# The hand-over to a recurrent stage: order of the early sigmoids, a PSUM bank, and who makes scale and shift

## The chip, the cores and the metric

The kernel runs on one core of a Trainium2 chip. The metric is device time in microseconds of one execution. A core has TensorE (PE, matrix products), VectorE (DVE), ScalarE (ACT, activations), GpSimd (POOL) and SyncE (SP, which issues transfers). Each engine works through its own queue in order. They meet through semaphores.

## The reference, cut to what matters

An image of 4 batches, 128 channels and 64 x 64 places passes an attention over places with a residual (layer 0), and then layer 1: a causal attention over 4096 tokens with layer norm, and a recurrent block. The change touches the recurrent block alone:

```
Wx   = layernorm(t) @ W.T                     # 4 batches x 4096 tokens x 128
Wx   = (Wx - mean) * rsqrt(var + 1e-5) * gamma + beta   # moments over all tokens of all batches
y    = 0
for each token:  y = sigmoid(Wx[token] + y @ V.T);  the output is t + y
```

## The kernel before

`fast_path` handles both layers. Nearly all of its time goes into the two attentions: products of scores (`s_ps`, L1062 and L1077), exponentials, products with values (`acc`, L1126 and L1137), one batch after another. The last block of the last batch is handled by `final_block`.

The recurrence is not run token by token. The 4096 tokens of a batch are cut into 256 chunks of 16 steps, and all chunks of a batch advance together: one step of one batch is one 128 x 256 product. A chunk's start is guessed: it is warmed up over the 9 tokens before it. Of these 9 steps, the first three (`AHEAD`) are "early": they run while the last block is still being finished, with moments over all blocks but the last one (`most`, made by `ahead`). The next six (`WARM`) and the 16 real steps use the moments over everything. At the end the kernel compares each chunk's guessed start with the true one and falls back to `general_path` if they differ.

An early step i of a batch has three instructions, each in a function of its own: `early_input` (L807: TensorE puts scale times Wx into PSUM), `early_product` (L812: adds V times the state), `early_sigmoid` (L820; for step 0 L822, straight from Wx). Batches 0, 1 and 2 take part whole, batch 3 without its last block (`WHOLE`). The last block's piece is 32 columns wide (`LAST`) and follows when its Wx is there. Results of early step 2 go to `warmed`, which lies in the tile `joint`. `early_place` says where in PSUM a step's sum lies: two tiles of two banks each, so four banks, with two halves of 256 columns in each. Before, a batch b uses bank b, and half i % 2 of it; the piece uses bank 3, and for step 2 bank 2.

The build makes an engine wait when another uses the same bank of PSUM, also for other columns of it.

`final_block` writes its order out by hand: `pin` keeps instructions in the order in which they are written. It mixes the early steps with the last block's own work: `normed_half`, `turned` (transposes), `product` (L994, with statistics at L995 on VectorE and a copy at L998 on ScalarE, which waits for these statistics).

After `final_block` come the moments over everything: `bn_aggr` (L1333), and `affine`, which makes the scale and the shift of the batch normalisation:

```
        nc.gpsimd.tensor_tensor(y, var, mhalf[:, :1], ALU.pow)
        nc.vector.scalar_tensor_tensor(z, in0=y, scalar=half, in1=y, op0=ALU.mult, op1=ALU.mult)
        nc.vector.scalar_tensor_tensor(y, in0=z, scalar=1.5, in1=y, op0=ALU.add, op1=ALU.mult)
        nc.vector.tensor_tensor(scale, y, gamma, ALU.mult)
        nc.vector.scalar_tensor_tensor(shift, in0=nmean, scalar=scale, in1=beta, op0=ALU.mult, op1=ALU.add)
```

GpSimd raises to the power -1/2, and one Newton step on VectorE makes it exact.

A later step of a batch is in `step`: a product `y_ps` (L1369; in step 0 L1374, in two parts, since the start of a chunk comes from the chunk before it), then VectorE's `z` = scale * Wx + y_ps (L1376), then ScalarE's sigmoid with the shift as its bias (L1380). Four batches are in flight. From step 1 on the order is pinned: batches 0 to 3, then the transposes for the output (`residual`, L1401) and the sums on GpSimd (`add`). The warm-up and step 0 are not pinned; a scheduler orders them at build time. `good` counts reciprocals that are in range; a copy of it into `count` (L1457) feeds the final verdict.

Of the kernel before, what the change touches and what calls it, by code (L numbers as in the profile page):

```python
# [9 lines left out]
F32 = mybir.dt.float32  # L10
AF = mybir.ActivationFunctionType
ALU = mybir.AluOpType
# [3 lines left out]
P = 128  # L16
# [3 lines left out]
BN_EPS = 1e-5  # L20
STEPS = 16
BY_C = 2
# [347 lines left out]
def fast_path(  # L370
# [22 lines left out]
    nc = tc.nc  # L393
    B, C, N = x.shape
# [101 lines left out]
    grid = lambda t: t.rearrange("p (g c) -> p g c", c=CPB)  # L496
    pin = tc.keep_in_program_order

    def affine(mv, pool, name, halved=True):

        one = lambda part: pool.tile([P, 1], F32, name=f"{name}_{part}")
        var, y, half, nmean, z = one("var"), one("y"), one("half"), one("nmean"), one("z")
        scale, shift, shift_half = one("scale"), one("shift"), halved and one("shift_half")
        nc.vector.tensor_scalar(var, mv[:, 1:2], BN_EPS, None, ALU.add)
        nc.gpsimd.tensor_tensor(y, var, mhalf[:, :1], ALU.pow)
        nc.vector.tensor_scalar(half, var, -0.5, None, ALU.mult)
        nc.vector.tensor_scalar(nmean, mv[:, 0:1], -1.0, None, ALU.mult)
        nc.vector.scalar_tensor_tensor(z, in0=y, scalar=half, in1=y, op0=ALU.mult, op1=ALU.mult)
        nc.vector.scalar_tensor_tensor(y, in0=z, scalar=1.5, in1=y, op0=ALU.add, op1=ALU.mult)
        nc.vector.tensor_tensor(scale, y, gamma, ALU.mult)  # L510
        if halved:
            nc.vector.scalar_tensor_tensor(
                shift_half, in0=nmean, scalar=scale, in1=beta_half, op0=ALU.mult, op1=ALU.add
            )
        nc.vector.scalar_tensor_tensor(shift, in0=nmean, scalar=scale, in1=beta, op0=ALU.mult, op1=ALU.add)
        return scale, shift, shift_half

# [10 lines left out]
    with tc.tile_pool(name="batch", bufs=1) as batch, tc.tile_pool(name="rows", bufs=2) as rowp, tc.tile_pool(  # L528
# [265 lines left out]
        def early_place(i, b, g0, g1):  # L794

            if not early:
                early.extend(halves.tile([P, 2, BLK], F32, tag="half", name="early") for _ in range(AHEAD - 1))
                early.extend(ps_s.tile([P, 2 * BLK], F32, tag="s", name="early_ps") for _ in range(2))
            cols = slice(g0 * CPB, g1 * CPB)
            bank, half = (b - 1, 1) if g0 and i == AHEAD - 1 else (b, i % 2)  # L800
            at = early[AHEAD - 1 + bank % 2][:, ds(bank // 2 * BLK + half * NCH, NCH)][:, cols]
            return cols, at, by_step[:, b, i - AHEAD - WARM + STEPS, g0:g1]

# [5 lines left out]
        def early_product(i, b, g0, g1):  # L809

            cols, at, _ = early_place(i, b, g0, g1)
            pin(nc.tensor.matmul(at, lhsT=vf, rhs=early_states(i - 1, b)[:, cols], start=False, stop=True))  # L812
# [125 lines left out]
        def final_block(b, g, agg, den):  # L938

            HALF = BLK // 2  # L940
            pair = lambda k: slice(2 * k, 2 * k + 2)
            token = lambda j: xs[:, b, ds(g * BLK + j * P, P)]
            own = folded(den, True, True)
            rec = recs[:, 1, b, ts(g, TPB)]
            pin(nc.vector.tensor_reduce(rec, own.rearrange("p q j -> p j q"), AX.X, ALU.add))
            pin(nc.vector.reciprocal(rec, rec))
            ops = [misc("o_ps"), misc("o_ps")]
            for j in range(TPB):
                pin(nc.tensor.matmul(ops[j // 2][:, ts(j % 2, P)], lhsT=agg[:, ts(j, P)], rhs=wv1, start=True, stop=True))

            st = stat.tile([P, TPB, nc.vector.BN_STATS_DIM], F32, tag="st", name="ln_st")
            mv = stat.tile([P, TPB, nc.vector.BN_AGGR_DIM], F32, tag="mv", name="ln_mv")
            var, y, half, z = (
                stat.tile([P, TPB], F32, tag=tag, name=f"ln_{tag}") for tag in ("var", "rstd", "half", "z")
            )
            for k in range(2):
                for j in range(2 * k, 2 * k + 2):
                    t = token(j)
                    pin(
                        nc.vector.scalar_tensor_tensor(  # L960
                            t, in0=ops[k][:, ts(j % 2, P)], scalar=rec[:, j : j + 1], in1=t, op0=ALU.mult, op1=ALU.add
                        )
                    )
                for j in range(2 * k, 2 * k + 2):
                    pin(nc.vector.bn_stats(st[:, j], token(j)))
                for j in range(2 * k, 2 * k + 2):
                    pin(nc.vector.bn_aggr(mv[:, j], st[:, j]))
                pin(nc.vector.tensor_scalar(var[:, pair(k)], mv[:, pair(k), 1], LN_EPS, None, ALU.add))
                pin(nc.gpsimd.tensor_tensor(y[:, pair(k)], var[:, pair(k)], mhalf[:, :2], ALU.pow))
                pin(nc.vector.tensor_scalar(half[:, pair(k)], var[:, pair(k)], -0.5, None, ALU.mult))  # L970
            by_tokens(b, g)

            xh = wk.tile([P, TPB, P], F32, tag="xh2", name="xh2")

            def normed_half(k):
                newton(y[:, pair(k)], half[:, pair(k)], z[:, pair(k)], True, True)
                j = 2 * k
                pin(nc.vector.tensor_scalar(xh[:, j], token(j), y[:, j : j + 1], None, ALU.mult))
                j += 1
                pin(nc.scalar.activation(xh[:, j], token(j), AF.Copy, scale=y[:, j : j + 1]))  # L980

            xhT = wk.tile([P, BLK], F32, tag="xhT2", name="xhT2")

            def turned(k):
                ps = misc("xh2T_ps")
                for i in range(2):
                    pin(nc.tensor.transpose(ps[:, ts(i, P)], xh[:, 2 * k + i], ident))
                pin(nc.vector.tensor_copy(xhT[:, ts(k, HALF)], ps[:, :HALF]))

            to = xs[:, b, ts(g, BLK)].rearrange("p (s c) -> p s c", s=STEPS)  # L990

            def product(k):
                wp = misc("wx_ps")[:, :HALF]
                pin(nc.tensor.matmul(wp, lhsT=wfc, rhs=xhT[:, ts(k, HALF)], start=True, stop=True))  # L994
                pin(nc.vector.bn_stats(ends[:, 3 + 6 * k : 9 + 6 * k], wp))  # L995
                part = pair(k)
                pin(
                    nc.scalar.copy(  # L998
                        to.rearrange("p s (q j u) -> p s q j u", q=Q, j=TPB)[:, :, :, part],
                        wp.rearrange("p (j q u s) -> p s q j u", q=Q, j=TPB // 2, s=STEPS),  # L1000
                    )
                )

            for part in WHOLE[:3]:
                early_step(1, part)
            normed_half(0)
            early_step(1, WHOLE[3])
            normed_half(1)
            early_step(2, WHOLE[0])
            turned(0)  # L1010
            early_input(2, *WHOLE[1])
            turned(1)
            early_product(2, *WHOLE[1])
            product(0)
            early_sigmoid(2, *WHOLE[1])
            early_input(2, *WHOLE[2])
            product(1)
            in_range(True)
            early_product(2, *WHOLE[2])
            early_input(2, *WHOLE[3])  # L1020
            early_product(2, *WHOLE[3])
            early_input(1, *LAST)
            early_input(2, *LAST)
            early_sigmoid(0, *LAST)
            for i in range(1, AHEAD):
                early_sigmoid(2, *WHOLE[1 + i])
                early_product(i, *LAST)
                early_sigmoid(i, *LAST)

# [279 lines left out]
    with tc.tile_pool(name="xr", bufs=1) as xrp, tc.tile_pool(name="y", bufs=2) as yp, tc.tile_pool(  # L1309
# [21 lines left out]

        mv = xrp.tile([P, nc.vector.BN_AGGR_DIM], F32, name="mv")
        nc.vector.bn_aggr(mv, ends)  # L1333
        scale, shift, _ = affine(mv, xrp, "all", False)
        start = xrp.tile([P, B, Q + 1, NCH // Q], F32, name="start")
        nc.gpsimd.memset(start[:, :, 0, 1:2], 0.0)
        ended = lambda b: start[:, b, 1:].rearrange("p q (g w) -> p g q w", g=NB)
# [58 lines left out]
        def residual(s):  # L1396
# [8 lines left out]
            pin(nc.vector.tensor_tensor(t, t, ps, ALU.add))  # L1405
            pin(nc.sync.dma_start(out=by_chunk(out_t)[:, :, s], in_=t))

        met = ps_m2.tile([P, BY_C, NCH], F32, name="met")
        gap = xrp.tile([P, B], F32, name="gap")
        tol = xrp.tile([P, B], F32, name="tol")  # L1410
# [4 lines left out]
        for s in range(-WARM, STEPS):  # L1415
            for b in range(B):
                step(b, s)
            if s >= 1:
                residual(s - 1)
            if TPB <= s < TPB + BY_C:  # L1420
                b = s - TPB
                pin(nc.scalar.copy(by_row(met[:, b]), ended(BY_C + b)))
            if 0 <= s < STEPS - 1:
                add(s)

# [27 lines left out]
        largest(1, second)  # L1453
        tc.mark_branch_hint_location(BRANCH, "LikelyTaken", engines=mybir.ALL_ENGINES)

        count = xrp.tile([P, B + 2], F32, name="count")
        nc.vector.tensor_copy(count[:, B:], good)  # L1457

        def judge():
            total = xrp.tile([P, 1], F32, name="total")  # L1460
# [87 lines left out]
```

## Time and profile before

| what | value |
|---|---|
| median of 3 runs | 2007.41 us (2006.56 to 2007.6) |
| the profiled execution | 2007.98 us, its span 2006.2 us |
| granted TensorE clock | 0.999 |
| TensorE busy | 1999.5 us (100% of the span) |
| VectorE, ScalarE, GpSimd busy | 1456.6, 974.5, 142.9 us |

The page gives busy time by engine, the chain of waits that ended last, and the costliest groups of instructions. A row of the timeline gives an instruction's start in us from the span's start, its length, engine, line and operands, how many were merged, and in brackets how long the engine stood idle before it and what ended that. PE and PEld are the product and the weight load of TensorE. A 32-bit product of 256 columns shows as two passes.

### The profile page before, as it was taken

Reading aid. Unit: us, or ns where it says so; the run is one execution under the profiler, and the core shown is the slowest. Engines: PE = TensorE matmul, PEld = TensorE weight load, DVE = VectorE, ACT = ScalarE, POOL = GpSimd, SP = SyncE. Lnnn points to the kernel's source line nnn. Section 1 sums busy time; section 2 is a strip of 40 time slices with the busy share of each in tenths; the row PEclk is TensorE's granted clock in tenths of the full one; section 3 lists DMA queues with packets and bytes.
Section 4 is the critical chain, followed back from the end, with each engine's and each line's share of the span. In section 5 each row is a group of like instructions: output and inputs, shape, how many; then the busy total and the mean of one; then the engine's idle time right before and its main releaser. Section 6 shows DMA issues by size and latency. Waiting matters only on the chain.

```text
span 2006.2 us, 31346 instructions
## 1 busy us (share of the span) xinstructions
PE 1999.5 (100%) x11862; PEld 873.2 (44%) x11862; DVE 1456.6 (73%) x2824; ACT 974.5 (49%) x1053; POOL 142.9 (7%) x253
## 2 busy tenths in 40 slices
PE   9999999999999999999999999999999999999999
PEld 3333354444333345444433334444443333544457
DVE  4799877555789987655588998664468998774469
ACT  5666633232666653333466664323356666333348
POOL 0000011000000001000000001000000000110016
PEclk9999999999999999999999999999999999999999
DMA  3111112310110111330102111222010111120018
GB/s 106 44 34 23 22 33 58 75 31 16 43 50 17 23 23 38 70 74 17 43 21 61 23 18 26 55 64 58 16 44 2 23 23 23 33 53 17 17 50 308
DMA packets 220027, 89.03 MB, mean 44 GB/s; under 512 B 142688, under 2 KB 204512, under 8 KB 219488
## 3 DMA queue, kind: packets, MB, share of 16 engines
q1 hardware_dynamic: 219584, 86.82, 17.5%
q8 instruction: 94, 1.54, 0.3%
q14 instruction: 61, 0.50, 0.1%
q10 hardware_dynamic: 288, 0.16, 0.0%
HBM read 45.84 MB, written 36.89 MB: 41 GB/s over the span
## 4 chain that ended last, share of the span: by engine, by line
PE 99%; DVE 0%; ACT 0%; issue 0%; POOL 0%; DVEq 0%; ACTq 0%; POOLq 0%
PE s_ps L1077 23%; PE acc L1137 22%; PE s_ps L1062 22%; PE acc L1126 22%; PE y_ps L1369 2%; PE o_ps L691 1%; PE r_ps L650 1%; PE kr_ps L587 1%; PE wx_ps L902 1%; PE v_ps L599 1%; PE o_ps L701 1%; PE yT_ps L1401 0%; PE early_ps L807 0%; PE warm_ps L544 0%; PE early_ps L812 0%; PE vT_ps L625 0%
## 5 line engine op out<-in xcount | busy, mean ns | idle before, releaser
L1106 DVE TENSOR_TENSOR dsum<-dsum,p 128x1024 f32<-128x1024 f32 x692 | 845.0, 1221 | 399.2 <-ACT p L1080 292.9
L1071 ACT ACTIVATE p<-s_ps,nshift 128x1024 f32<-128x1024 f32 x512 | 570.1, 1117 | 310.3 <-PE s_ps L1062 279.4
L1080 ACT ACTIVATE p<-s_ps 128x1024 f32<-128x1024 f32 (+2 forms) x288 | 274.5, 953 | 605.0 <-PE s_ps L1077 581.1
L1126 PE MATMUL acc<-p,v 64*64 64x512 f32 x4096 | 527.9, 589 | 0.0
L1062 PE MATMUL s_ps<-kr 64*64 64x512 f32 x2048 | 522.6, 590 | 0.0
L1062 PE MATMUL s_ps<-kr,swap 64*64 64x512 f32 x2048 | 522.6, 590 | 0.0
L1077 PE MATMUL s_ps<-rows,xhT 128*128 128x512 f32 (+3 forms) x1152 | 500.4, 558 | 0.0
L1137 PE MATMUL acc<-p,xh 128*128 128x512 f32 (+3 forms) x1152 | 500.2, 557 | 0.0
L1077 PEld LDWEIGHTS s_ps<-rows,xhT 128*128 128x128 f32 x1152 | 215.2, 190 | 243.1 <-issue 202.4
L1137 PEld LDWEIGHTS acc<-p,xh 128*128 128x128 f32 x1152 | 216.1, 190 | 239.8 <-issue 223.4
L1126 PEld LDWEIGHTS acc<-p,v 64*64 64x64 f32 x4096 | 156.6, 133 | 282.8 <-issue 274.6
L1062 PEld LDWEIGHTS s_ps<-kr,swap 64*64 64x64 f32 x2048 | 141.5, 133 | 140.6 <-issue 132.7
L1062 PEld LDWEIGHTS s_ps<-kr 64*64 64x64 f32 x2048 | 141.5, 133 | 134.6 <-issue 132.3
L729 POOL TENSOR_TENSOR ln_rstd<-ln_var,mhalf 128x4 f32<-128x4 f32 x63 | 67.9, 1079 | 1178.8 <-DVE ln_var L727 1178.7
L1114 DVE TENSOR_TENSOR dsum<-dsum,p 128x256 f32<-128x256 f32 (+1 forms) x120 | 55.8, 498 | 61.5 <-POOL p L1086 61.5
L715 DVE SCALAR_TENSOR_TENSOR xs<-o_ps,recs,xs 128x128 f32<-128x128 f32 x252 | 69.5, 343 | 4.6 <-PE o_ps L701 1.7
L738 DVE TENSOR_SCALAR xh<-xs,ln_mv,ln_rstd 128x128 f32<-128x128 f32 x252 | 70.2, 342 | 2.0
L724 DVE BATCH_NORM_STATS2 ln_st<-xs 128x6 f32<-128x128 f32 x252 | 61.8, 272 | 0.0
L1086 POOL TENSOR_SCALAR_AFFINE_SELECT p<-p 128x128 f32<-128x128 f32 x128 | 34.6, 294 | 353.3 <-ACT p L1080 348.8
L1104 DVE COPY dsum<-p 128x1024 f32<-128x1024 f32 x44 | 30.2, 686 | 30.3 <-ACT p L1080 15.4
L752 DVE STREAM_TRANSPOSE sqT<-xh 128x512 f32<-128x512 f32 x63 | 44.7, 709 | 1.7
L661 DVE TENSOR_REDUCE part<-sq 128x16 f32<-128x512 f32 x64 | 41.6, 670 | 0.8
(172 smaller groups left out, 872.5 us busy)
## 6 DMA issues: line engine op xcount, KB each, us to landing
xs<-in_xT SPq DMA_DIRECT2D x32, 256.0 KB, 3.4
by_r<-sqT SPq DMA_DIRECT2D x128, 64.0 KB, 2.2
xhT<-by_r SPq DMA_DIRECT2D x128, 64.0 KB, 2.0
chans<-sqT SPq DMA_DIRECT2D x124, 64.0 KB, 1.8
xhT<-chans SPq DMA_DIRECT2D x31, 256.0 KB, 2.8
xs<-in_x SPq DMA_DIRECT2D x12, 512.0 KB, 5.3
x2c<-sqT SPq DMA_DIRECT2D x80, 64.0 KB, 1.8
swap<-kr SPq DMA_DIRECT2D x32, 128.0 KB, 2.3
```

Of the source, the lines that this page charges most:

```text
L715: nc.vector.scalar_tensor_tensor(t, in0=op[:, ts(j, P)], scalar=rec[:, j : j + 1], in1=t, op0=ALU.mult, op1=ALU.add)
L724: nc.vector.bn_stats(st[:, j], xs[:, b, ds(g * BLK + j * P, P)])
L729: nc.gpsimd.tensor_tensor(y, var, mhalf, ALU.pow)
L738: nc.vector.tensor_scalar(dst[:, j], xs[:, b, ds(g * BLK + j * P, P)], mv[:, j, 0:1], y[:, j : j + 1], ALU.subtract, ALU.mult)
L1062: ins = nc.tensor.matmul(ps[c * M : c * M + M, ts(r, BLK)], lhsT=keys[:, ts(c, M)], rhs=rows[r], start=True, stop=True,)
L1071: nc.scalar.activation(it.p, ps, AF.Exp, bias=nshift)
L1077: nc.tensor.matmul(ps[:, off : off + n], lhsT=lhsT, rhs=rhs, start=True, stop=True)
L1080: ins = nc.scalar.activation(it.p[:, :off], ps[:, :off], AF.Exp, scale=float(P) ** -0.5)
L1106: nc.vector.tensor_tensor(flat, flat, it.p, ALU.add)
L1114: nc.vector.tensor_tensor(den[:, h, q0:], den[:, h, q0:], it.p[:, o : o + n], ALU.add)
L1126: ins = nc.tensor.matmul(bt.acc[c * M : c * M + M, r], lhsT=bt.v[part, m * TPB + j, h], rhs=it.p[part, ts(c, BLK)], start=it.first, stop=i ...
L1137: ins = nc.tensor.matmul(bt.acc[:, 0, q0:], lhsT=bt.xh[:, t], rhs=it.p[:, o : o + n], start=it.first and h == 0, stop=it.last and h == 1,)
```

## The change

It has three parts.

1. In `final_block`, early sigmoids of step 2 move directly behind their products: batch 1's stands ahead of `product(0)` instead of behind it, batch 2's directly behind its product, and batch 3's ahead of the piece's later steps. The piece's inputs are no longer issued ahead of its step-0 sigmoid. In `early_place` the piece's step 1 lies in bank 0 instead of bank 3 (half 1); step 2 stays in half 1 of bank 2.
2. The final scale and shift are made without `affine`: GpSimd multiplies its power by gamma (`steep`), VectorE's Newton step then ends in the scale itself, and ScalarE makes the shift with an Identity activation (scale and bias from tiles). `affine` loses its switch `halved`.
3. The copy of `good` into `count` moves from VectorE to ScalarE, pinned in step 6.

The diff:

```diff
-    def affine(mv, pool, name, halved=True):
+    def affine(mv, pool, name):
...
-            bank, half = (b - 1, 1) if g0 and i == AHEAD - 1 else (b, i % 2)
+            bank, half = (b - 1 if i == AHEAD - 1 else 0, 1) if g0 else (b, i % 2)
...
             early_product(2, *WHOLE[1])
+            early_sigmoid(2, *WHOLE[1])
             product(0)
-            early_sigmoid(2, *WHOLE[1])
             early_input(2, *WHOLE[2])
             product(1)
             in_range(True)
             early_product(2, *WHOLE[2])
+            early_sigmoid(2, *WHOLE[2])
             early_input(2, *WHOLE[3])
             early_product(2, *WHOLE[3])
-            early_input(1, *LAST)
-            early_input(2, *LAST)
             early_sigmoid(0, *LAST)
+            early_sigmoid(2, *WHOLE[3])
             for i in range(1, AHEAD):
-                early_sigmoid(2, *WHOLE[1 + i])
+                early_input(i, *LAST)
                 early_product(i, *LAST)
                 early_sigmoid(i, *LAST)
...
-        scale, shift, _ = affine(mv, xrp, "all", False)
+        one = lambda part: xrp.tile([P, 1], F32, name=f"all_{part}")
+        var, y, half, nmean, z = one("var"), one("y"), one("half"), one("nmean"), one("z")
+        steep, scale, shift = one("steep"), one("scale"), one("shift")
+        nc.vector.tensor_scalar(var, mv[:, 1:2], BN_EPS, None, ALU.add)
+        nc.gpsimd.tensor_tensor(y, var, mhalf[:, :1], ALU.pow)
+        nc.gpsimd.tensor_tensor(steep, y, gamma, ALU.mult)
+        nc.vector.tensor_scalar(half, var, -0.5, None, ALU.mult)
+        nc.vector.tensor_scalar(nmean, mv[:, 0:1], -1.0, None, ALU.mult)
+        nc.vector.scalar_tensor_tensor(z, in0=y, scalar=half, in1=y, op0=ALU.mult, op1=ALU.mult)
+        nc.vector.scalar_tensor_tensor(scale, in0=z, scalar=1.5, in1=steep, op0=ALU.add, op1=ALU.mult)
+        nc.scalar.activation(shift, nmean, AF.Identity, scale=scale, bias=beta)
...
+        count = xrp.tile([P, B + 2], F32, name="count")
...
+            if s == TPB + BY_C:
+                pin(nc.scalar.copy(count[:, B:], good))
...
-        count = xrp.tile([P, B + 2], F32, name="count")
-        nc.vector.tensor_copy(count[:, B:], good)
```

More of the change, by code (lines that the diff above doesn't have):

```diff
@@ L497, in fast_path @@
     pin = tc.keep_in_program_order
-    def affine(mv, pool, name, halved=True):
+    def affine(mv, pool, name):
         one = lambda part: pool.tile([P, 1], F32, name=f"{name}_{part}")
         var, y, half, nmean, z = one("var"), one("y"), one("half"), one("nmean"), one("z")
-        scale, shift, shift_half = one("scale"), one("shift"), halved and one("shift_half")
+        scale, shift, shift_half = one("scale"), one("shift"), one("shift_half")
         nc.vector.tensor_scalar(var, mv[:, 1:2], BN_EPS, None, ALU.add)
@@ L510, in affine @@
         nc.vector.tensor_tensor(scale, y, gamma, ALU.mult)
[L511 to L514, printed above, removed]
+        nc.vector.scalar_tensor_tensor(
+            shift_half, in0=nmean, scalar=scale, in1=beta_half, op0=ALU.mult, op1=ALU.add
+        )
         nc.vector.scalar_tensor_tensor(shift, in0=nmean, scalar=scale, in1=beta, op0=ALU.mult, op1=ALU.add)
```

## The prediction

> **What bounds the kernel now.** I read the page's engine shares first, then the chain of waits, then the timeline of each engine between 1949 and 1972 us, where every edit of the change lies.
>
> ```profile
> PE 1999.5 (100%) x11862; PEld 873.2 (44%) x11862; DVE 1456.6 (73%) x2824; ACT 974.5 (49%) x1053; POOL 142.9 (7%) x253
> ...
> PE 99%; DVE 0%; ACT 0%; issue 0%; POOL 0%; DVEq 0%; ACTq 0%; POOLq 0%
> ```
>
> TensorE is busy all the time and carries the chain. The change removes no matmul, so it can win or lose only TensorE's idle moments around one hand-over. The chain shows the place:
>
> ```profile
> 1952.49 0.37 ACT xs L998
> 1952.87 0.39 ACT joint L820
> 1953.25 0.04 issue
> 1953.30 0.65 PE early_ps L807 x2
> ...
> 1956.00 10.14 PE y_ps L1369 x44
> 1966.14 1.91 PE y_ps L1374 x16
> 1968.05 1.88 PE y_ps L1369 x8
> 1969.93 0.33 PE yT_ps L1401 x3
> 1970.26 1.73 PE y_ps L1369 x8
> ```
>
> Two regimes follow the hand-over. From step 1 on (1968 us) a step costs 1.73 us of products and 0.33 of transposes, 2.06 us, and TensorE never waits: a shift of its first steps arrives undiminished at the end. In the warm-up (the 44-pass row) it does wait. The list of waits for 1956 to 1966 us has one line on it:
>
> ```profile
> PEld y_ps L1369 <- ACT y L1380: 1.0, 5, 0.2
> ```
>
> Read instruction by instruction, batch 3's products start at 1956.37, 1958.22, 1960.03, 1961.84, 1963.66 and 1965.47 us, its step 0 near 1967.42 and its step 1 at 1969.30. So a warm-up sweep lasts 1.81 us, though its four products fill only 4 x 2 passes x 0.216 = 1.73. The 1.81 is one batch's loop: a pass of 0.29 that waited for its weights, 0.38 for the second pass, 0.48 of z (L1376), 0.51 of sigmoid (L1380), and 0.15 of hand-overs. **Batch 3, the last to start, is the one waited for.**
>
> ScalarE's timeline at the hand-over (start, length, line, what it writes and reads, and in brackets the idle time before it):
>
> ```profile
> 1954.72 0.47 ACT L820 ACTIVATE joint<-early_ps,most_shift 128x256 f32<-128x256 f32 x1 [0.59 <-PE early_ps L807]
> 1955.10 0.28 ACT L820 ACTIVATE early<-early_ps,most_shift 128x32 f32<-128x32 f32 x1
> 1955.27 0.45 ACT L820 ACTIVATE joint<-early_ps,most_shift 128x224 f32<-128x224 f32 x1
> 1956.03 0.29 ACT L820 ACTIVATE joint<-early_ps,most_shift 128x32 f32<-128x32 f32 x1 [0.32 <-PE early_ps L812]
> ```
>
> VectorE's timeline, with the small operations that make scale and shift and the first z behind them:
>
> ```profile
> 1954.39 0.22 DVE L508 SCALAR_TENSOR_TENSOR all_z<-all_y,all_half 128x1 f32<-128x1 f32 x1 [0.34 <-POOL all_y L505]
> 1954.64 0.16 DVE L509 SCALAR_TENSOR_TENSOR all_y<-all_z,all_y 128x1 f32<-128x1 f32 x1
> 1954.83 0.16 DVE L510 TENSOR_TENSOR all_scale<-all_y,gamma 128x1 f32<-128x1 f32 x1
> 1955.03 0.22 DVE L515 SCALAR_TENSOR_TENSOR all_shift<-all_nmean,all_scale,beta 128x1 f32<-128x1 f32 x1
> 1955.53 0.87 DVE L1376 SCALAR_TENSOR_TENSOR z<-xs,all_scale,y_ps 128x256 f32<-128x256 f32 x2 [0.28 <-PE y_ps L1369]
> ```
>
> The first z starts at 1955.53, 0.28 after the shift: what came last was its product (until 1955.42), not the affine numbers.
>
> **What the Trainium skill says.** "PSUM — Partial Sum Buffer", section "PSUM bank collisions raise a hardware error", says to guard PSUM by bank and quadrant rather than by address. The trace agrees with that as the build's habit: the 0.59 us wait above is for a matmul into other columns of the bank being read. "ScalarE: Activation LUTs", section "What ACT_TABLE_LOAD costs", puts an ACTIVATE with immediates at 186 ns, each [128,1] pointer operand at about 93 ns more, and the per-element part at 0.833 ns. This trace's 32-column rows give 0.41 us with two pointers (L822) and 0.28 with one. The section "Table sets: the hidden batching unit" says that identity is in every set; no run shows Identity yet.
>
> **The change part by part**, on the clock of this profile. Line numbers are those before.
>
> *Sigmoids.* The step-2 sigmoid of batch 1 waits in ScalarE's queue behind the copy that ends the statistics' read (1952.49). Moved ahead, it can start at its product's end, 1951.56 instead of 1952.76. The two copies (L998) stay where the statistics release them, 1952.49 and 1953.31. Batch 2's sigmoid then runs at 1953.58 instead of 1954.72, the last piece's step-0 sigmoid at 1953.98 (0.26 later, now behind it), and batch 3's at 1954.30 instead of 1955.27. TensorE loses its 0.22 us stall at L807 (1953.30 back to 1953.08).
>
> *The built order moves more than the diff says.* Before, TensorE issues warm-up products as batches 0, 1, 2, 3, then the second sweep. After, it issues batch 0, the last piece's step 1, batches 1 and 2, the last piece's step 2, then **batches 0 and 1 of the second sweep, and only then batch 3 of the first**. That order, 0, 1, 3, 2, stays through the warm-up. ScalarE's order likewise puts the last piece's final sigmoid behind the first two warm-up sigmoids.
>
> *Batches 0 to 2.* Batch 0's product: 1953.84 to 1954.43 instead of 1954.74 to 1955.42. The last piece's step-1 product must wait for its step-0 sigmoid (until 1954.39) and ends near 1954.94. Batch 1's product ends at 1955.45 (1955.86 before), batch 2's at 1955.88 (1956.51 before).
>
> *Scale and shift.* On VectorE four small instructions go (0.16 + 0.16 + 0.22 + 0.16 for the count's copy) and one of 0.16 replaces them. GpSimd's multiplication follows all_y, which ends at 1954.35. Its size is not in the trace: it is bounded by 0.10 (the 128x1 memset) and 0.55 (the 128x1 power). I take 0.25, from the line through the adds of 128x128 (0.535) and 128x512 (1.544): an intercept of 0.20, plus its start. It then ends near 1954.67. The scale is ready at 1954.87 instead of 1954.99; with 0.55 it would be 1955.17. Four wait instructions in front of the first z took about 0.3 us in this trace and now follow the scale, not the shift: z at **1955.09 instead of 1955.53, 0.44 earlier**. The shift on ScalarE, two pointers and one element, I take as 0.41 - 31 x 0.833 ns = 0.385: 1954.91 to 1955.29, 0.04 later than before, and hidden because the first sigmoid waits for z until 1955.57. What stands behind it is the last piece's step-1 sigmoid: 1955.20 to 1955.48, still before TensorE reaches the piece's step-2 input at 1955.72. First warm-up sigmoid: 1955.69 instead of 1956.26.
>
> *Batch 3.* The last piece's step-2 product ends at 1956.25. Its sigmoid is behind two warm-up sigmoids (1955.69 and 1956.10), so it runs 1956.51 to 1956.80 instead of 1956.03 to 1956.32. TensorE takes batch 0's second sweep at 1956.28 (its sigmoid ends 1956.20), batch 1's at 1956.79, and batch 3's first at **1957.22 instead of 1956.37, 0.85 later**. Even a free GpSimd multiplication leaves 1957.0, because batch 1's product stands behind the last piece's.
>
> *The way out.* Each batch still needs six sweeps at 1.81. Batch 3 is due at 1957.22 + 5 x 1.81 = 1966.3 for its sixth; I take 1966.4. Between its sixth sweep and its step 0 TensorE has only batch 2's step 0 (0.46) to do, and batch 3's step 0 can start only 1.87 later, near 1968.29: some **0.9 us of idle TensorE that did not exist before**. This returns the lead that batches 0 to 2 gained. Step 1's first three products (1.30) then hide most of the next loop, and step 1 of batch 3 starts at 1970.1 instead of 1969.3. Sum: **+0.8 us**. From there nothing has slack.
>
> *At no cost:* the count's copy on ScalarE in step 6 (estimate 0.19 us, two elements with immediates). It lies beside TensorE's 2.06 us step, in which ScalarE idles 0.35 us; the met copies of 0.36 us lie in steps 4 and 5 already, and those steps last 2.06 too. SP's queue issues the same transfers in the same order.
>
> Against the profiled execution's own 2007.98 us (span 2006.2 and 1.8 around it) this makes 2008.8. The median of the runs shown is 0.57 lower, so I forecast 2007.41 + 0.8 = **2008.2 us**. Within 0.2% means 4.0 us either way, about what a measurement of this kernel can tell from no change.
>
> **The rivals.** *The earlier start carries through:* if batch 3's late place cost nothing, the end would move with the first z and sigmoid, by 0.44 to 0.57: 2006.9. For it speak the stalls removed; against it, that batch 3 paces the warm-up now and starts later.
>
> *A slow GpSimd multiplication:* at 0.55 us it delays the scale by 0.3 more and everything behind it: 2008.5.
>
> *A table switch, the one that ends slower:* if Identity were not in the sigmoids' set, ScalarE would load a table ahead of the shift and another behind it. Here an ACT_TABLE_LOAD took 1.28 us (L822): two are 2.57, and 5.3 with the drain that the skill's page adds (2.66 per switch). With the 0.8 this gives 2010.8 to 2013.5; it decides from 4.0 us in all. Against it: the built order has no load between the step-0 sigmoids and the end, and Copy runs among sigmoids already.
>
> *That the change doesn't do what it says:* if the first z still waited for its product and not the scale, the gain of 0.44 would go and batch 3 would still start last: 2008.3 to 2008.7.
>
> **How the numbers follow.** Main case with its variants (slow multiplication, no gain): 0.82, all within 0.2%. Earlier start carried through: 0.13, within too. Table switch: 0.02, about half of it beyond 4 us. Something unseen: 0.03, with a gain or loss above 4 us for most. That gives faster 0.01, same 0.96, slower 0.03. The runs of before span 1.04 us, so the main case's own range is 2007.4 to 2009.1; reaching to the carried-through case and to a larger idle at the way out makes 2006.7 to 2009.4.
>
> **What would show it.** Right: first z near 1955.1, batch 3's first warm-up product near 1957.2, after two products of batches 0 and 1; a gap of about 0.9 us on TensorE between 1967 and 1968.3; batch 3's step 1 near 1970.1; steps of 2.06 from there; an all_shift row of about 0.39 on ScalarE without a table load. Wrong: step 1 starting before 1969.3, a second ACT_TABLE_LOAD after 1953, or steps longer than 2.06.

## The result, and the profile after

| | before | after |
|---|---|---|
| median of 22 runs | 2007.26 us (2006.45 to 2007.91) | 2010.67 us (2007.42 to 2011.95) |
| the profiled execution | 2007.98 us | 2010.48 us |
| its span | 2006.2 us | 2005.6 us |
| time less span | 1.8 us | 4.9 us |

The changed kernel takes 1.0015 times as long, with a 95% interval of 1.0009 to 1.0021. The medians lie 3.4 us apart; 0.8 was forecast. The last row of the table is the surprise: the profiled span is *shorter* than before, and the execution longer. Most of what was lost lies behind the last instruction. Over the 22 runs after the change the span has a median of 2006.05 us; the median time before, less 1.8, is 2005.5. So some 0.6 us of the 3.4 lie inside the span, an estimate from these figures.

**Inside the span.** The page's shares and the chain's shares, first of all:

```profile
PE 1998.3 (100%) x11862; PEld 873.1 (44%) x11862; DVE 1455.8 (73%) x2821; ACT 974.4 (49%) x1055; POOL 143.8 (7%) x254
...
PE 99%; DVE 0%; ACT 0%; DMA 0%; issue 0%; POOL 0%; DVEq 0%; SPq 0%; POOLq 0%; ACTq 0%
```

VectorE has three instructions fewer, ScalarE two more, GpSimd one more (254 instead of 253): that one will matter. TensorE still carries the chain.

The two profiles need a common zero. The copy of the last block's first product on ScalarE (line 998 before, 997 after) starts at 1952.49 us before and at 1951.38 after. I don't put that 1.1 us down to the change: nine kernels below that differ from the one before only by spare instructions at the start have the same copy anywhere from 1951.40 to 1952.74. So I count from this copy. From it to the first transposes of the steps these nine, the kernel before and the third part of the change alone all take 17.24 to 17.27 us, so a difference of a tenth can be read. The end varies too: from the last transposes to the end of the span it is 6.24 us before, 5.84 after, and 5.80 to 6.08 in the nine. The chain of waits after the change:

```profile
1953.27 0.25 DVE all_z L1341
...
1954.02 0.36 DVE z L1385
1954.38 0.20 issue
1954.59 0.52 ACT y L1389
1955.10 0.04 issue
1955.15 9.25 PE y_ps L1378 x40
1964.40 0.60 PE y_ps L1383 x4
...
1966.57 0.41 ACT start L1389
1966.98 0.04 issue
1967.02 0.77 PE y_ps L1383 x4
1967.79 1.88 PE y_ps L1378 x8
1969.67 0.33 PE yT_ps L1410 x3
1970.00 1.73 PE y_ps L1378 x8
```

Before, the chain went through TensorE without a break from 1956 us on. Now it leaves TensorE once, for one batch's sigmoid `start` at 1966.57, and comes back at 1967.02 for the four products of step 0. TensorE's timeline shows both ends of that gap, batch 3's late first warm-up product (`joint`) and the idle time it leads to:

```profile
1955.15 1.13 PE L1378 MATMUL y_ps<-y,vf 128*128 128x256 f32 x4
1956.11 0.59 PE L1378 MATMUL y_ps<-joint,vf 128*128 128x256 f32 x2
...
1967.02 0.77 PE L1383 MATMUL y_ps<-start,vf 128*128 128x128 f32 x4 [0.69 <-ACT start L1389]
```

Two passes of batches 0 and 1 each (`y`) stand ahead of batch 3's `joint`. Before, the eight passes of all four batches' first products (`joint`) stood ahead of the second sweep:

```profile
1954.74 1.11 PE L1369 MATMUL y_ps<-joint,vf 128*128 128x256 f32 x4
...
1955.83 1.24 PE L1369 MATMUL y_ps<-joint,vf 128*128 128x256 f32 x4
1956.91 9.23 PE L1369 MATMUL y_ps<-y,vf 128*128 128x256 f32 x40
```

ScalarE's and VectorE's timelines show the new way to scale and shift:

```profile
1953.14 0.44 ACT L819 ACTIVATE joint<-early_ps,most_shift 128x224 f32<-128x224 f32 x1
1953.81 0.39 ACT L1343 ACTIVATE all_shift<-all_nmean,beta,all_scale 128x1 f32<-128x1 f32 x1 [0.23 <-DVE all_scale L1342]
1954.11 0.27 ACT L819 ACTIVATE early<-early_ps,most_shift 128x32 f32<-128x32 f32 x1
1954.59 0.91 ACT L1389 ACTIVATE y<-z,all_shift 128x256 f32<-128x256 f32 x2 [0.21 <-ACT early L819]
1955.40 0.27 ACT L819 ACTIVATE joint<-early_ps,most_shift 128x32 f32<-128x32 f32 x1
```

```profile
1953.27 0.24 DVE L1341 SCALAR_TENSOR_TENSOR all_z<-all_y,all_half 128x1 f32<-128x1 f32 x1 [0.34 <-POOL all_y L1337]
1953.62 0.16 DVE L1342 SCALAR_TENSOR_TENSOR all_scale<-all_z,all_steep 128x1 f32<-128x1 f32 x1
1954.02 1.26 DVE L1385 SCALAR_TENSOR_TENSOR z<-xs,all_scale,y_ps 128x256 f32<-128x256 f32 x3 [0.25 <-DVE all_scale L1342]
```

No table load stands around the shift, and what ended the wait before z is now the scale. The piece's last sigmoid (1955.40) stands behind two warm-up sigmoids.

**Behind the span.** The view of transfers between 2002 and 2012 us counts, beside data, packets that fetch instructions (queue and kind, packets, MB, share). Before:

```profile
q14 instruction: 3, 0.02, 1.0%
q8 instruction: 1, 0.02, 0.8%
```

After:

```profile
q8 instruction: 2, 0.03, 2.1%
q14 instruction: 7, 0.06, 1.9%
```

Three on queue 14 and one on queue 8 lie inside the span in both kernels (starting at 2004.65 to 2005.01 us before, 2004.21 to 2004.36 after), about a microsecond after the engines jump over the fallback and while they work off the last barrier. The other four and one stand only in the trace after the change. The view from 2006.8 to 2012 us has them alone:

```profile
q8 instruction: 1, 0.02, 2.2%
q14 instruction: 4, 0.03, 2.2%
```

They start between 2008.40 and 2008.72, and the last ends at 2010.57. That is 2.8 to 5.0 us behind the last instruction, and the DMA share of the stretch in between (2005.7 to 2008.3) is 0.00. This second round ends close to the end of the execution (4.9 us behind the span). It is no proof of a cause: an execution that is over 1.8 us behind its span, as before, ends ahead of the place where such a round would start, so its trace can't show whether one would follow.

Time less span of all 22 runs after the change falls into two groups: 17 runs of 4.6 to 5.2 us (median 4.9) and 5 of 1.7 to 1.9. Those 5 have a median time of 2008.01 us, 0.75 above the median before. In the 181 runs of the kernel before that accompany the experiments below, time less span is 1.7 to 1.9 in every one.

### The profile page after: what moved, and what is told of

It is laid out like the page before. It is cut to its first block, busy times and chain, and to the rows that moved or that the text cites. A ratio compares the mean times of both kernels' runs of the same rounds, so it can differ in the third digit from the quotient of the medians.

```text
span 2005.6 us, 31347 instructions
## 1 busy us (share of the span) xinstructions
PE 1998.3 (100%) x11862; PEld 873.1 (44%) x11862; DVE 1455.8 (73%) x2821; ACT 974.4 (49%) x1055; POOL 143.8 (7%) x254
## 4 chain that ended last, share of the span: by engine, by line
PE 99%; DVE 0%; ACT 0%; DMA 0%; issue 0%; POOL 0%; DVEq 0%; SPq 0%; POOLq 0%; ACTq 0%
PE s_ps L1076 23%; PE acc L1136 22%; PE s_ps L1061 22%; PE acc L1125 22%; PE y_ps L1378 2%; PE o_ps L690 1%; PE r_ps L649 1%; PE wx_ps L901 1%; PE kr_ps L586 1%; PE v_ps L598 1%; PE o_ps L700 1%; PE yT_ps L1410 0%; DMA xs<-in_x 0%; PE early_ps L806 0%; PE early_ps L811 0%; PE vT_ps L624 0%
```

## The experiments

**Theory 1:** the extra time lies behind the span and comes from the length of GpSimd's stream of instructions, which one added instruction, whatever it does, takes to a bad place. The built program has 447 instructions for GpSimd before and 448 after, of 64 bytes each (28,672 bytes after). **Theory 2:** the length of VectorE's or ScalarE's stream, which change too (8700 to 8698, 9421 to 9423). **Theory 3:** what happens in the last 50 us, the moved copy of the count or the order of the early sigmoids.

### One spare GpSimd instruction in the kernel before

```diff
     nc.gpsimd.memset(point5, 0.5)
+    spare = const.tile([P, 1], F32, name="spare")
+    for _ in range(1):
+        nc.gpsimd.memset(spare, 0.0)
```

> The kernel before with one spare GpSimd memset of a [128,1] tile among the constants at the start, nothing else. It makes GpSimd's stream of instructions 448 long instead of 447, as in the changed kernel. Theory 1 (the changed kernel's missing 2.6 us lie behind the span, and come from the length of GpSimd's stream): span unchanged near 2006.2, but time less span about 4.9 us instead of 1.8 in most runs, so about 2009.9 to 2010.4 in the median. Theory 2 (VectorE's or ScalarE's stream decides, both are as before here): time less span 1.8, about 2007.3. Theory 3 (the order of the last 50 us decides): 2007.3 as well.

Measured: 2010.10 us against 2007.57 of the kernel before, ratio 1.001 [1.0003, 1.0016]. Time less span is 4.5 to 5.1 in 17 of 21 runs, 1.7 to 1.8 in 4. The span is untouched (2006.0). The view of transfers from 2002 to 2012 us:

```profile
q14 instruction: 7, 0.06, 1.9%
q8 instruction: 2, 0.03, 1.9%
```

The same seven and two as after the change. An instruction that took about 0.1 us, 2000 us before the end, adds 2.5 us to the median. Theories 2 and 3 fall: neither of their causes is in this kernel.

### The three parts of the change alone

The second part alone (scale and shift; GpSimd 448):

```diff
-        scale, shift, _ = affine(mv, xrp, "all", False)
+        nc.gpsimd.tensor_tensor(steep, y, gamma, ALU.mult)
...
+        nc.scalar.activation(shift, nmean, AF.Identity, scale=scale, bias=beta)
```

> Only the second part of the change: GpSimd multiplies by gamma, ScalarE makes the final shift; sigmoids, bank and count as before. GpSimd's stream is 448 long, VectorE's one shorter (8699), ScalarE's one longer (9422). Theory 1: time less span about 4.9 us in most runs. Theory 2 (VectorE at 8698 or ScalarE at 9423 needed): 1.8. Theory 3 (count copy or timing of the end): 1.8. The span itself: between 0.4 less (earlier scale) and 0.8 more (a late batch 3) than 2006.2; that part is small here because all_shift stands ahead of the piece's sigmoids in ScalarE's order.

Measured: 2011.02 us (before 2007.57), ratio 1.0016 [1.0009, 1.0023]; time less span 4.5 to 5.3 in 19 of 21 runs.

The first part alone (sigmoids and bank; GpSimd 447):

```diff
-            bank, half = (b - 1, 1) if g0 and i == AHEAD - 1 else (b, i % 2)
+            bank, half = (b - 1 if i == AHEAD - 1 else 0, 1) if g0 else (b, i % 2)
...
+            early_sigmoid(2, *WHOLE[1])
             product(0)
-            early_sigmoid(2, *WHOLE[1])
```

> Only the first part of the change: the sigmoids' order in the last block and the bank; scale, shift and count as before. GpSimd's stream is 447 long as before, VectorE's one shorter (8699). Theory 1: time less span 1.8 us in every run; the span about 0.3 to 0.9 over 2006.2, since batch 3's warm-up comes later in the built order; total about 2007.6 to 2008.2. Theory 2 (VectorE's stream decides): time less span about 4.9, total about 2011. Theory 3 (order of the early sigmoids): 2010.7, as with the whole change.

Measured: 2008.07 us (before 2007.57), ratio 1.0001 [0.9992, 1.0009]; time less span 1.7 to 1.9 in all 13 runs.

The third part alone (count; GpSimd 447):

```diff
+            if s == TPB + BY_C:
+                pin(nc.scalar.copy(count[:, B:], good))
...
-        nc.vector.tensor_copy(count[:, B:], good)
```

> Only the third part of the change: the count's copy on ScalarE in step 6. GpSimd's stream is 447 long as before, VectorE's one shorter (8699), ScalarE's one longer (9422). Theory 1: time less span 1.8 us, total as before, 2007.3 within 0.3. Theory 2 (VectorE's or ScalarE's stream decides): time less span about 4.9, total about 2010.4. Theory 3 (what the verdict at the end waits for, so this copy, decides): 2010.4.

Measured: 2007.27 us (before 2007.57), ratio 0.9997 [0.9989, 1.0006]; time less span 1.7 to 1.9 in all 13 runs. No cost of the count's copy is seen, as forecast.

So only the part that adds a GpSimd instruction brings the added time behind the span. Inside the span the parts do not add up. From the copy to the first transposes of the steps it is 17.27 us before, 17.89 with the order alone, 18.09 with scale and shift alone, and 18.13 with all. Either part alone makes the build issue batch 3's first sweep late, and once it is late the other adds little.

### The changed kernel with one GpSimd instruction fewer

```diff
-        nc.gpsimd.memset(tol[:, 0:1], TOL**4)
-        nc.gpsimd.memset(tol[:, B - 1 :], TOL**4)
+        nc.gpsimd.memset(tol[:, 0 :: B - 1], TOL**4)
```

> The changed kernel with one GpSimd instruction fewer: the two memsets that write the first and the last column of tol become one with a stride. GpSimd's stream is 447 long again; nothing else changes on any engine. Theory 1 (the length of GpSimd's stream makes the 3 us behind the span): time less span 1.8 us in every run; the total is 0.8 above the kernel before, which is what the span's own changes cost: about 2008.2. Rival (the second of GpSimd's two operations at the hand-over, or ScalarE's shift, does it in some other way): time less span 4.8 in most runs, about 2010.7.

Measured: 2007.90 us (before 2007.52), ratio 1.0003 [0.9994, 1.0011]; time less span 1.7 to 1.8 in all 13 runs. Merging two memsets of a 4-column tile takes some 2.8 us off the changed kernel (2010.67 to 2007.90, from different sets of runs). What stays, 0.4 us in the medians, can't be told from nothing by these runs. In the profile the loss inside the span is still there: from the copy to the first transposes it is 18.15, as after the change.

### Other lengths

Spare instructions at the start of the kernel before, of GpSimd (two memsets for 449; for the longer ones a memset and a chain of multiplications of one column by itself), and once four of VectorE.

```diff
+    nc.gpsimd.memset(spare, 1.0)
+    for _ in range(64):
+        nc.gpsimd.tensor_tensor(spare, spare, spare, ALU.mult)
```

> The kernel before with two spare GpSimd memsets (two columns of a spare tile) at the start: GpSimd's stream is 449 long. If only the exact length 448 (a multiple of 64) is dear: time less span 1.8 us, about 2007.5. If everything from 448 on is dear (another stretch of instructions has to be fetched at the end): time less span 4.8 in most runs, about 2010.1.

> The kernel before with four spare VectorE memsets at the start: VectorE's stream is 8704 long instead of 8700, a multiple of 64 like GpSimd's 448. If every engine's stream pays at such a length: time less span above 1.8, by up to 3 us. If it is GpSimd's alone, or depends on something that VectorE's end doesn't share: 1.8, total 2007.5 as before.

> The kernel before with 65 spare GpSimd instructions at the start, so that GpSimd's stream is 512 long (four times 128; 448 and 449 were dear, 447 was not). If being at or past 448 is dear without end: time less span 4.8. If the dear range is one stretch of 64: time less span 1.8. The span itself may begin otherwise by some tenths, since the spare instructions take about 2 to 7 us of GpSimd at the start.

> The kernel before with 129 spare GpSimd instructions at the start, so that GpSimd's stream is 576 long (4.5 times 128, as 448 is 3.5 times). If what counts is the place within 128: time less span 4.8 as at 448, whatever 512 gives. If past 448 everything is dear: 4.8, with 512 at 4.8 as well. If only one stretch behind 448 is dear: 1.8.

> The kernel before with spare GpSimd instructions at the start, one fewer than in the kernel of length 512: GpSimd's stream is 511 long. If the dear lengths are the whole upper half of each 128 (448 to 511, and from 576 on): time less span 4.8 us in nearly all runs, about 2010. If only lengths close behind a multiple of 64 are dear (448 and 449 of 128 x 3 + 64, and 576): 1.8, about 2007.1.

> The kernel before with spare GpSimd instructions at the start, GpSimd's stream 455 long. Of this stream the jump over the fallback leaves some 14 instructions (two, the last barrier's eight, four at the very end). If it is dear when the 448th place falls among these last ones (dear from 448 to about 461): time less span 4.8 us in most runs. If only 448 and 449 themselves are dear: 1.8.

> The same with a stream of 462. By the account in which the 448th place must fall among the last 14 or so instructions, this is just past the dear lengths: time less span 1.8, and the fetch of GpSimd's last stretch stands beside those of the other engines (four packets on queue 14 instead of three at the jump). If the dear lengths reach further (to 480, half way to 512): 4.8.

> The same with a stream of 472. By the account of the last 14 or so instructions: time less span 1.8. If the dear lengths reach to 480 or beyond: 4.8.

Measured, with the changed kernel and its variants for comparison:

| GpSimd's length | kernel | time less span, us | runs above 4.4 | median time, us |
|---|---|---|---|---|
| 447 | before; order alone; count alone; changed with 447 | 1.7 to 1.9 | none | 2007.3 to 2008.1 |
| 447, VectorE 8704 | before, four VectorE memsets | 1.7 to 1.9 | 0 of 13 | 2007.44 |
| 448 | before, one spare | 1.7 to 5.1 | 17 of 21 | 2010.10 |
| 448 | changed kernel | 1.7 to 5.2 | 17 of 22 | 2010.67 |
| 449 | before, two spare | 4.5 to 5.4 | 21 of 21 | 2010.43 |
| 455 | before, spare | 1.7 to 1.8 | 0 of 11 | 2007.18 |
| 462 | before, spare | 1.7 to 1.8 | 0 of 11 | 2007.04 |
| 472 | before, spare | 1.7 to 1.8 | 0 of 11 | 2006.94 |
| 511 | before, spare | 1.7 to 1.9 | 0 of 11 | 2007.26 |
| 512 | before, spare | 1.7 to 1.9 | 0 of 11 | 2007.04 |
| 576 | before, spare | 1.7 to 5.1 | 7 of 11 | 2009.48 |

The dear lengths, those at which most runs have 4.5 us or so behind the span, are a narrow place, not a threshold: 448 and 449, not 447 and not 455; and again 128 further on at 576, but not at 512. Against the kernel before in the same sets of runs, the ratio is 1.0014 [1.0007, 1.002] at 449. At 576 it is 1.0006 [0.9998, 1.0015], which by itself tells no difference; there it is the time less span that shows it. Several of my expectations fell on the way. Dear "from 448 on without end", dear in "one upper half of each 128" and dear while the 448th place lies among the last 14 instructions (455) are all wrong. VectorE's stream at 8704, a multiple of 64 and of 128, pays nothing.

The fetches at the jump fit this. The view of transfers from 2002 to 2012 us at length 455:

```profile
q14 instruction: 4, 0.03, 1.1%
q8 instruction: 1, 0.02, 0.9%
```

All five now come at the jump, one more on queue 14 than in the kernel before. These counts are of one profiled execution for each kernel. At 447 there are three and one at the jump. At 455, 462, 472, 511 and 512 there are four and one at the jump. At 448, 449 and 576, each profiled in a dear execution, there are three and one at the jump, and then a whole round of five behind the span. The packets on queue 14 carry 8.2 KB each (61 packets and 0.50 MB on the page before), which is 128 instructions of 64 bytes: the distance from 448 to 576. The reading that fits is that a stretch of GpSimd's instructions begins at the 448th place and again 128 further on: below it nothing of it is needed, well above it is fetched at the jump with the others, and when only the very last instructions of GpSimd lie in it, it is asked for too late. This is argued, not shown: the packets do not name their engine, and that the fourth is GpSimd's is inferred from the counts. 448 is three and a half times 128, and why a stretch should begin there is open, as is what fills the 2.8 us ahead of the second round. What is shown is the tie between the length of GpSimd's stream and the time behind the span. Where between 449 and 455 the dear place ends wasn't tried.

### Batch 3 earlier

The other question is whether batch 3's late place really makes the 0.8 us inside the span. Two kernels, both the changed one at length 447, have the order written out. In the first, the piece's step-0 sigmoid stands ahead of batch 2's step-2 sigmoid, the piece's step 1 behind batch 3's early product, and its step 2 between the first warm-up products of batches 1 and 2; the second sweep comes behind all four:

```diff
             product(1)
+            early_sigmoid(0, *LAST)
...
+            early_step(1, LAST)
             early_sigmoid(2, *WHOLE[3])
...
+        for b in range(B):
+            if b == 2:
+                early_step(2, LAST)
+            opened.append(ps_y.tile([P, NCH], F32, tag=f"y{b}", name="y_ps"))
+            pin(nc.tensor.matmul(opened[b], lhsT=vf, rhs=prev[b], start=True, stop=True))
```

> The changed kernel with GpSimd's stream at 447, and with the order at the hand-over written out: the piece's step-0 sigmoid ahead of batch 2's sigmoid, its step 1 behind batch 3's product, then the warm-up products of batches 0 and 1, the piece's step 2, the products of batches 2 and 3, and only then the second sweep; on ScalarE the shift, then the piece's last sigmoid, then the first warm-up sigmoid. Theory (batch 3's late first product costs the 0.8 us of the span): from the first copy of the last block's product on ScalarE to batch 3's step 1 it took 16.81 us before and 17.59 after; here batch 3's first product comes about 0.4 us earlier than before, so about 16.4; time less span 1.8; total about 0.3 to 0.5 below the kernel before. Rival (the late start of batch 3 is not what paces; the warm-up itself became longer, for instance by waits between GpSimd, VectorE and ScalarE): 17.3 or more, total 0.5 or more above the kernel before.

Measured: 2007.55 us (before 2007.52), ratio 1.0001 [0.9993, 1.0009]; time less span 1.7 to 1.9 in all 13 runs. From the copy to the first transposes it is 17.76, better than the changed kernel's 18.15 but 0.5 worse than before: a miss. TensorE's timeline shows where it went:

```profile
1952.92 0.54 PE L811 MATMUL early_ps<-early,vf 128*128 128x224 f32 x2
1954.01 0.41 PE L806 MATMUL early_ps<-xs,near 128*128 128x32 f32 x2 [0.55 <-ACT joint L819]
...
1955.79 1.24 PE L1428 MATMUL y_ps<-joint,vf 128*128 128x256 f32 x4
```

The piece's step-1 input (128x32) waited 0.55 us for ScalarE's read of batch 2's sum. They lie in different banks, 0 and 2, but in one tile: `early_ps` is two tiles of two banks each. The build keeps them apart by tile, which is wider than the "bank" that the section on the kernel before speaks of. The second kernel puts the piece's step 1 into the other tile, and its step 2 behind batch 0's product:

```diff
-            bank, half = (b - 1 if i == AHEAD - 1 else 0, 1) if g0 else (b, i % 2)
+            bank, half = (b - 1 if i == AHEAD - 1 else 1, 1) if g0 else (b, i % 2)
...
-            if b == 2:
+            if b == 1:
                 early_step(2, LAST)
```

> The earlier written-out order once more, with the wait that it ran into taken away: there the piece's step 1 lay in the same two-bank tile as batch 2's sum and waited 0.55 us for batch 2's sigmoid. Here it lies in bank 1, in the other tile, whose last reader is done, and its step 2 comes behind batch 0's first warm-up product. GpSimd's stream is 447 long. Theory (batch 3's first product sets the way out): the second pass of that product starts 3.9 to 4.0 us after the first copy of the last block's product, against 4.20 before and 4.95 in the changed kernel, and the first transposes of the steps follow 13.1 us behind it as in all kernels so far: 17.0 to 17.1 after the copy, against 17.27 before. Time less span 1.8; total 0.2 to 0.3 below the kernel before. Rival (something else in the warm-up gets longer as soon as batch 3 comes early): 17.25 or more, total as before or above.

Measured: 2007.02 us against 2007.33 before. The ratio is 0.9999 [0.9991, 1.0007], which tells no difference; time less span is 1.7 to 1.9 in all 13 runs. In the profile the forecast holds: 17.07 us from the copy to the first transposes. TensorE's timeline has no such wait left, and all six passes of batches 1 to 3 in one row:

```profile
1953.04 0.31 PE L806 MATMUL early_ps<-xs,near 128*128 128x32 f32 x2
1953.39 0.41 PE L811 MATMUL early_ps<-early,vf 128*128 128x32 f32 x2
...
1954.51 1.54 PE L1430 MATMUL y_ps<-joint,vf 128*128 128x256 f32 x6
```

Put side by side, counted in us from the copy:

| kernel | second pass of batch 3's first product | first transposes | between them |
|---|---|---|---|
| order written out, other tile | 3.97 | 17.07 | 13.09 |
| before | 4.20 | 17.27 | 13.07 |
| order written out, same tile | 4.69 | 17.76 | 13.07 |
| first part alone | 4.72 | 17.89 | 13.17 |
| second part alone | 4.91 | 18.09 | 13.18 |
| changed kernel | 4.95 | 18.13 | 13.18 |
| changed kernel, length 447 | 4.96 | 18.15 | 13.19 |

From batch 3's first product on the way is 13.1 us in every kernel of the table, whatever stands ahead of it, and from the first transposes to the last it is 30.24 us in all. When z starts (2.64 to 3.30 us behind the copy) does not order the kernels; batch 3 does. The order written out with the other tile is the best version found, by 0.2 us in the profile; its median of 2007.02 us against 2007.33 can't tell it from the kernel before.

## Why the prediction was wrong, and where it was right

**The step that failed** is the sum against the whole time: "Against the profiled execution's own 2007.98 us (span 2006.2 and 1.8 around it) this makes 2008.8." The 1.8 was carried over as a constant. It is 4.9 in most runs after the change. In these 17 runs it adds 3.1 us; the median thus comes to 2010.67 instead of 2008.2, beyond the range's upper end of 2009.4. The 5 runs without it have a median of 2008.01, and the changed kernel at length 447 has 2007.90.

**The term that was mis-sized** is the price of the added GpSimd instruction. I bounded its 128x1 multiplication between 0.10 and 0.55 us and took 0.25. On GpSimd it took 0.19 us, and 0.27 from the end of `all_y` (1953.23) to its own end:

```profile
1952.69 0.55 POOL L1337 TENSOR_TENSOR all_y<-all_var,mhalf 128x1 f32<-128x1 f32 x1 [4.54 <-DVE all_nmean L1340]
1953.31 0.19 POOL L1338 TENSOR_TENSOR all_steep<-all_y,gamma 128x1 f32<-128x1 f32 x1
```

That was right. As one more instruction in GpSimd's stream it cost 3.1 us elsewhere, in 17 of 22 runs; the kernel before with one spare memset shows that the count of instructions does it and not the multiplication. None of my rivals had this, and the share of 0.03 for "something unseen" was all there was for it. The forecast that the change stays within 0.2% holds for the measured ratio, though with little to spare. That 4.0 us is "about what a measurement of this kernel can tell from no change" was wrong: the interval of 1.0009 to 1.0021 tells 3.4 us from nothing.

**Inside the span, step by step**, counted from the copy:

| step | forecast | measured |
|---|---|---|
| first z | 2.60 | 2.64 |
| shift on ScalarE, its length | 0.385 | 0.387 |
| first warm-up sigmoid | 3.20 | 3.21 |
| batch 3's first product, first pass | 4.73 | 4.73 |
| TensorE's idle time before batch 3's step 0 | 0.9 | 0.69 |
| step 1 of batch 3 | 17.6 | 17.59 |

The sum of +0.8 us comes out as 18.13 - 17.27 = 0.86. The idle time was mis-sized by 0.2, without effect on the end. The written-out orders show, in the profiles, that the cause was the one named: batch 3, the last to start, is the one waited for. The shift's length can be set beside the price in the Trainium skill's "ScalarE: Activation LUTs", section "What ACT_TABLE_LOAD costs": 186 ns, 93 for each of two pointer operands and 0.8 for one element make an estimate of 0.373 us, and 0.387 was measured.

**The rivals.** "The earlier start carries through" fell: z starts 0.39 us earlier and the steps 0.86 later. "A slow GpSimd multiplication" fell with its 0.19 us. "A table switch" fell: the shift's row stands between two sigmoids' rows without a load, so Identity was in the loaded set, as that page's section "Table sets: the hidden batching unit" says. "The change doesn't do what it says" fell as well: the wait before z now ends with the scale.

**A reading of mine that needs mending:** I spoke of banks of PSUM that the build guards. The first of the written-out orders shows a wait of 0.55 us between two banks of one tile. For the changed kernel itself this made no difference: there batch 2's sum had been read (until 1952.95) before the piece's step-1 input (1953.16).

## What to carry to other kernels

Take the whole time less the span, run by run, before reading a difference from the rows of a profile: here that subtraction shows that no row inside the span can hold the 3.1 us. Where the tail jumps by about 3 us, count GpSimd's instructions in the built program and try one more or one fewer; here a merged memset took back 2.8 us of 3.4. Only this program and these lengths were tried. And in a stage with several chains in flight, ask which chain starts last, not which starts first: its first product alone set the end, to within 0.12 us, in seven kernels.

## What was unexpected in the hardware

A spare 0.1 us memset on GpSimd at the start of a 2007 us program makes it end 2.5 us later in the median, all of it behind its last instruction. In the profiled executions a second round of instruction fetches stands there; whether it is the cause or comes with it is open. The added time depends on the length of GpSimd's stream in a narrow place (448, 449 and 576 are dear; 447, 455, 462, 472, 511 and 512 are not), and at 448 not in every execution (17 of 21 and 17 of 22), while at 449 it was in all 21. VectorE's stream at 8704 did not show it.
